# Two attention blocks on one core: row sums taken for two stretches at a time, and three smaller moves

## The chip, the cores and the metric

The kernel runs on one core of a Trainium2 chip. The metric is the device time in microseconds (us), median of the runs shown. The core has TensorE (PE), VectorE (DVE), ScalarE (ACT), GpSimd (POOL) and SyncE (SP), which here only issues DMAs. PE writes its results to PSUM[...] and DVE or ACT take them out. All data are fp32.

## The reference

Two residual attention blocks over `x` of shape (8, 512, 32, 32), 1024 tokens to an image.

```python
# layer 0: 32 groups, 8 heads of 64 channels
h = group_norm(x, gn_weight, gn_bias)
qkv = einsum('oc,bct->bot', w_qkv, h) + b_qkv
weight = softmax(einsum('bct,bcs->bts', q * scale, k * scale))
a = einsum('bts,bcs->bct', weight, v)
x = x + einsum('oc,bct->bot', w_proj, a) + b_proj
# layer 1: 8 groups, one head of 512 channels
xn = group_norm(x, gamma, beta)
attn = softmax(einsum('bqc,bck->bqk', q, k) * 512**-0.5)
x = x + conv1x1(attn applied to v, p_w, p_b)
```

## The kernel before

The images are worked through one after another. The period of an image is some 350 us. It holds the attention of layer 0 (`attention0`), the projection of layer 0, layer 1 of the image before (`layer1_scores`, `layer1_rest`), and the values, keys and queries of layer 0 for the image after. The 512 x 512 products use a seven-product scheme instead of eight (`wino`, `inner_steps`), whose sums and differences of factors are made by DVE and POOL.

**Attention of layer 0.** The eight heads are taken in four pairs `hp`, and the 1024 queries in two halves `tb`; pair and half make a stretch, eight to an image. The halves come in the order 0, 1, for the last pair 1, 0. In a stretch PE makes eight score tiles `sc` (128 keys, two heads, 512 queries). Each takes two PSUM banks of one of three pools, in turn (`ps_pools[n % 3]`). ACT takes the exponential to `e`, and DVE adds the eight `e` to a running sum `total` (called `sum` in the profile): the first add is line 623, the six others line 625. Then PE multiplies the `e` with the values into `av`, and ACT copies `av` to `a` without scaling it.

**Row sums.** `reciprocals` (line 575) is called right after. Four matmuls with a 128 x 32 block of ones sum `total` over the partitions (`sums`, 256 columns for four blocks of queries in four quadrants of the partitions). DVE makes the reciprocals from PSUM (line 586) and keeps their minimum in `low_recs` (line 587). POOL adds them to `all_recs` (line 588); both are looked at once, at the end of the kernel. Then SP's queue stores the reciprocals to DRAM (line 590) and reads them back in two broadcasts (line 600). POOL scales `a` with them (line 644); in the last stretch of an image that is done by DVE, and ACT's queue takes the DMAs. `av` and `sums` share a pool of two banks (`ps_acc`). The tiles `rc` and `r` have two buffers each.

**Order of the work.** All matmuls are pinned to the order of the text. The other engines' instructions are put in order by a planner, unless pinned too; with equal readiness the earlier in the text comes first. Short steps of other stages are handed to the stretches in lists (`extra`, one before and one after `av`): factors of the image for the next product (`t_h`, `h`, `t_a`) on DVE, and norms on ACT. In other stages short steps lie in a queue, `background`, from which each product takes one to four.

**Layer 1's scores** (`scores1`) are seven products of seven steps. Each puts its `small` steps in the queue: the steps `gsteps` of the factors of the scores, the 12 statistics `stats` of the projected image (eight half tiles, four ends), and `add_up`, POOL's sums of the exponentials.

**Keys and queries.** `keys_and_queries` runs `conv2` for keys, then for queries; each has four parts that take a list of hooks. The mean over groups (`group_mean`, a matmul of four columns and four small DVE instructions) and the scale (`affine`, one more such matmul, then DVE and POOL) are for the norm of a later image, whose statistics the values' stage makes.

Of the kernel before, what the change touches and what calls it, by code (L numbers as in the profile page):

```python
# [9 lines left out]
F32 = mybir.dt.float32  # L10
I32 = mybir.dt.int32
AF = mybir.ActivationFunctionType
ALU = mybir.AluOpType
AX = mybir.AxisListType

P = 128
# [13 lines left out]
def two_attention_blocks_kernel(  # L30
# [8 lines left out]
    nc = tc.nc  # L39
    B, C, T = x.shape  # L40
    KC = C // P
# [24 lines left out]
    def matmul(*args, **kw):  # L66
        tc.keep_in_program_order(nc.tensor.matmul(*args, **kw))  # L67
# [4 lines left out]
    def pcols(name):  # L72
        i = 4 * PARAMS.index(name)
        return par[:, i : i + 4]
# [101 lines left out]
    def main_path(ctx):  # L176
# [11 lines left out]
        def pair_tile(name):  # L188
            return big_tile(name, (P, 2, HT))

        def acc_tile(name):
            return ps_acc.tile([P, HT], F32, tag="acc", name=name)
# [379 lines left out]
            return out  # L572


        def reciprocals(total, uid, across, queue=nc.sync):

            sums = acc_tile(f"sums_{uid}")[:, : 2 * P].rearrange("p (a b) -> p a b", a=2)
            for i in range(4):
                matmul(sums[ts(i, 32), :, :], ones[:, :32], total[:, :, ts(i, P)], start=True, stop=True)
            rc = rpool.tile([P, 2, P], F32, tag="rc", name=f"rc_{uid}")
            nc.vector.reciprocal(rc, sums)  # L586
            nc.vector.tensor_tensor(low_recs, low_recs, rc, ALU.min)
            nc.gpsimd.tensor_tensor(all_recs, all_recs, rc, ALU.add)  # L588
            rows = rowpool.tile([2, 4, P], F32, tag="rows", name=f"rows_{uid}")
            queue.dma_start(rows.rearrange("j i n -> i j n"), rc[0:P:32, :, :])  # L590
            if across:
                r = pair_tile(f"r_{uid}")
                for j in range(2):
                    row = rows[j : j + 1].rearrange("j i n -> j (i n)")
                    queue.dma_start(r[:, j, :], row.to_broadcast([P, HT]))
            else:
                r = rpool.tile([P, HT], F32, tag="r", name=f"r_{uid}")
                for j in range(2):
                    row = rows[j : j + 1].rearrange("j i n -> j (i n)")
                    queue.dma_start(r[ts(j, 64), :], row.to_broadcast([64, HT]))  # L600
            return r


        def attention0(b, q, k, v, a, extra):
            n = 0

            for hp in range(KC):
                for tb in (0, 1) if hp < KC - 1 else (1, 0):
                    uid = f"0_{b}_{hp}_{tb}"
                    total = pair_tile(f"sum_{uid}")  # L610
                    es = []
                    for s in range(NS):
                        sc = ps_pools[n % 3].tile([P, 2, HT], F32, tag="sc", name=f"sc_{uid}_{s}")
                        n += 1
                        for j in range(2):
                            matmul(
                                sc[:, j, :], k[hp][ts(j, 64), ts(s, P)], q[hp][ts(j, 64), ts(tb, HT)],
                                start=True, stop=True,
                            )
                        e = pair_tile(f"e_{uid}_{s}")  # L620
                        nc.scalar.activation(e, sc, AF.Exp, scale=(C // 8) ** -0.5)  # L621
                        if s == 1:
                            nc.vector.tensor_add(total, es[0], e)  # L623
                        elif s > 1:
                            nc.vector.tensor_add(total, total, e)  # L625
                        es.append(e)
                    for f in extra.pop(0) if extra else ():
                        f()
                    av = acc_tile(f"av_{uid}")
                    for s in range(NS):  # L630
                        for j in range(2):
                            matmul(
                                av[ts(j, 64), :], v[s // 2][:, s % 2, hp * P + j * 64 : hp * P + (j + 1) * 64],
                                es[s][:, j, :], start=(s == 0), stop=(s == NS - 1),
                            )
                    for f in extra.pop(0) if extra else ():
                        f()
                    dst = a[hp][:, ts(tb, HT)]
                    nc.scalar.copy(dst, av)  # L639

                    last = (hp, tb) == (KC - 1, 0)
                    r = reciprocals(total, uid, False, nc.scalar if last else nc.sync)
                    if not last:
                        nc.gpsimd.tensor_tensor(dst, dst, r, ALU.mult)  # L644
                    else:
                        scaled = lambda dst=dst, r=r: tc.keep_in_program_order(nc.vector.tensor_mul(dst, dst, r))

            assert not extra
            return scaled


        def scores1(f, gf, gsteps, first, uid, stats):
# [26 lines left out]
            def exps(r, c):  # L679
                for cc in (1, 0):  # L680
                    nc.scalar.activation(e[c, cc, r], e[c, cc, r], AF.Exp, scale=scale)  # L681
# [11 lines left out]
            def product(s, p, y, x, before, small, after7=(), final=()):  # L693
                def mm(ps, j, start):
                    for i in range(2):
                        matmul(
                            ps[:, i, :], f[p][j][:, ts(i, P)], g2[p][j], start=start and i == 0, stop=True, skip_group_check=True
                        )

                def extra(r, cc, read, written):  # L700

                    if p == 6 and written:
                        more((0, 1), (1, 0), (1, 1), r, cc)
                    if p == 7 and written:
                        more((1, 1), (1, 0), (1, 1), r, cc)

                inner_steps(
                    f"{uid}_{s}", s % 2, 2, mm, add, lambda *at: blocks(y, *at), x and (lambda *at: blocks(x, *at)),
                    extra, after7, final, [lambda: background.extend(small), *(lambda q=q: factors(q) for q in before)],
                )  # L710

            product(0, 1, (1, 0), None, [2], stats[:3] + gsteps[:2])
            product(1, 2, (0, 0), (1, 0), [5], gsteps[2:4], (), [lambda: exps(0, 0)])
            product(2, 5, (1, 1), None, [6, 4], gsteps[4:] + stats[3:6])
            product(3, 6, (1, 0), (1, 0), [7, 3], stats[6:7])
            product(4, 7, (1, 0), (1, 0), [], stats[7:9])
            product(5, 3, (0, 1), (0, 1), [], stats[9:11] + add_up(0, 0), [lambda: exps(1, 1)], [lambda: exps(0, 1)])
            product(
                6, 4, (1, 0), (1, 0), [], stats[11:] + add_up(1, 1) + add_up(0, 1), (),
                [lambda: exps(1, 0), lambda: background.extend(add_up(1, 0) + steps)],  # L720
            )

# [229 lines left out]

        def keys_and_queries(b, f, norm, hooks):

            k = conv2("k", f, None, f"k0_{b}", hooks)
            hooks = [[all_background], [], []]
            if norm:
                hooks[1].append(lambda: norm.group_mean(acc_tile(f"gmean_0_{b + 1}")[:, :KC]))
                hooks[2].append(lambda: norm.affine(acc_tile(f"gvar_0_{b + 1}")[:, :KC]))
            q = conv2("q", f, pcols("bq0"), f"q0_{b}", hooks)  # L960
            return q, k

        def layer1_scores(b, inner):
# [9 lines left out]
        def layer1_rest(b, inner, gf, gsteps, stats, hooks, ahead):  # L973
            first = query_factors(gf[1], f"1_1_{b}")
            total, ef = scores1(inner, gf, gsteps, first, f"1_{b}", stats)
            state = {}

            def sums():
                state["r"] = reciprocals(total, f"1_{b}", True)

            z = by_token(
                weight("z"), hf, f"z1_{b}", hooks=[*hooks, [sums]], back=3,
                after=[load_weight, lambda: background.extend(zsteps)],
            )
            all_background()
            xt = [load_again(b, c, "x") for c in range(KC)]
            stiles = [big_tile(f"sz{i}_{b}", (P, 2, 2, C // 2)) for i in (1, 2, 4)]
            halves = lambda t: (t[:, :, : C // 2], t[:, :, C // 2 :])
            zf, zsteps = left_sums(
                [halves(t) for t in z[:2]], [halves(t) for t in z[2:]],  # L990
                [lambda j, t=t: t[:, j, :, :] for t in stiles], nc.vector.tensor_add, nc.vector.tensor_sub,
            )
            values1(b, zf, ef, state["r"], xt, f"1_{b}", ahead)
# [274 lines left out]
```

## Time and profile before

| what | us |
|---|---|
| median of 3 runs | 2849.69 (2848.17 to 2850.7) |
| the profiled execution | 2849.52 |
| its span, first to last instruction | 2847.7 |
| one stretch of attention, from sums to sums | 14.66 |
| PE busy in the span | 2827.0 (99%) |
| DVE busy | 2083.8 (73%) |
| POOL busy | 1205.4 (42%) |
| ACT busy | 929.0 (33%) |

Times in a timeline are counted from the start of the span. A line of it gives the start, the time, the engine, the line, the operation, what is written from what, and in brackets the idle time of the engine before it and what ended that. In a line of groups the two numbers behind the bar are the busy time in us and the mean of one in ns, then the idle time before. An fp32 matmul stands in the records as two instructions. Matmuls overlap in the records, so PE's pace is read from the starts.

### The profile page before, as it was taken

The numbers are of one execution on the slowest core, as the hardware profiler recorded it, in microseconds if no ns is written. First come the engines' busy times: TensorE is split into PE (matmuls) and PEld (weight loads), VectorE is DVE, ScalarE is ACT, GpSimd is POOL, SyncE is SP. The second block draws the span as 40 slices with busy tenths as digits, with TensorE's granted clock in tenths as the row PEclk, the third lists the DMA queues.
The fourth block names the chain that finished last, engine by engine and source line by source line (L and its number), as shares of the span: only waits on it lengthen the run. The fifth ranks groups of instructions, "written<-read, shape, count | busy, mean of one in ns | idle before, by whom it ended". The sixth has DMA issues, their size and how long they took to land.

```text
span 2847.7 us, 32456 instructions
## 1 busy us (share of the span) xinstructions
PE 2827.0 (99%) x11846; PEld 1690.0 (59%) x11846; DVE 2083.8 (73%) x2733; ACT 929.0 (33%) x1177; POOL 1205.4 (42%) x1193
## 2 busy tenths in 40 slices
PE   9999999999999999999999999999999999999998
PEld 5435635866367653677537674376743868338584
DVE  5587787766877678776787757877578775887765
ACT  1252452214522145220552215422154311633130
POOL 2123215732167321673227722277123761147672
PEclk9999999999999999999999999999999999999999
DMA  8632403133031230322213232122311223012301
GB/s 276 190 127 90 180 20 126 36 144 134 20 144 65 106 128 26 134 94 97 109 49 111 94 118 92 49 108 97 134 72 49 107 101 142 35 52 94 121 2 68
DMA packets 91597, 280.59 MB, mean 99 GB/s; under 512 B 10595, under 2 KB 36387, under 8 KB 82470
## 3 DMA queue, kind: packets, MB, share of 16 engines
q1 hardware_dynamic: 89638, 276.15, 26.7%
q10 hardware_dynamic: 1792, 2.29, 0.2%
q8 instruction: 96, 1.57, 0.2%
q14 instruction: 71, 0.58, 0.1%
HBM read 227.31 MB, written 51.09 MB: 98 GB/s over the span
## 4 chain that ended last, share of the span: by engine, by line
PE 97%; DVE 2%; issue 1%; ACT 0%; POOL 0%; DVEq 0%; POOLq 0%; ACTq 0%
PE sc L67 16%; PE av L67 16%; PE psb_av L67 6%; PE psb L67 5%; PE psa_av L67 4%; PE psc_av L67 4%; PE psc L67 3%; PE psa L67 3%; PE psb_z L67 3%; PE psb_p L67 3%; PE psb_v L67 3%; PE psb_k L67 3%; PE psb_g L67 3%; PE psb_q L67 2%; PE psa_p L67 2%; PE psa_z L67 2%
## 5 line engine op out<-in xcount | busy, mean ns | idle before, releaser
L625 DVE TENSOR_TENSOR sum<-sum,e 128x1024 f32<-128x1024 f32 x384 | 522.4, 1360 | 41.8 <-DVE sum L623 1.4
L621 ACT ACTIVATE e<-sc 128x1024 f32<-128x1024 f32 x512 | 476.8, 1053 | 73.2 <-PE sc L67 72.3
L67 PE MATMUL sc<-q,k 64*128 64x512 f32 x2048 | 458.7, 596 | 0.5
L67 PE MATMUL av<-e,v 128*64 128x512 f32 x2048 | 453.6, 596 | 0.0
L67 PEld LDWEIGHTS sc<-q,k 64*128 64x128 f32 x2048 | 193.3, 186 | 239.2 <-ACT e L621 104.0
L67 PEld LDWEIGHTS av<-e,v 128*64 128x64 f32 x2048 | 141.4, 137 | 304.3 <-issue 304.3
L588 POOL TENSOR_TENSOR all_recs<-all_recs,rc 128x256 f32<-128x256 f32 x72 | 65.2, 905 | 528.3 <-DVE rc L586 520.7
L644 POOL TENSOR_TENSOR a<-a,r 128x512 f32<-128x512 f32 x56 | 112.6, 2010 | 265.0 <-DMA r<-rows 220.8
L586 DVE RECIPROCAL rc<-sums 128x256 f32<-128x256 f32 x72 | 126.4, 1756 | 46.4 <-PE sums L67 26.5
L532 POOL TENSOR_TENSOR k<-k,k 128x256 f32<-128x256 f32 x28 | 20.0, 727 | 315.8 <-DVE u_k L527 315.8
L639 ACT COPY a<-av 128x512 f32<-128x512 f32 x64 | 37.4, 585 | 318.2 <-PE av L67 318.2
L623 DVE TENSOR_TENSOR sum<-e,e 128x1024 f32<-128x1024 f32 x64 | 78.5, 1226 | 58.9 <-ACT e L621 58.9
L67 PE MATMUL psb<-inner,inner_h 128*128 128x256 f32 x448 | 116.1, 382 | 1.2 <-DVE u L671 0.5
L67 PE MATMUL psa_av<-e,z 128*128 128x512 f32 x256 | 113.3, 596 | 0.0
L140 ACT ACTIVATE h<-h,b,s 128x1024 f32<-128x1024 f32 x62 | 78.4, 1268 | 93.9 <-DMA h<-in_x 77.3
L411 POOL TENSOR_TENSOR inner_h<-h,inner_h 128x256 f32<-128x256 f32 x120 | 106.8, 892 | 2.2
L67 PEld LDWEIGHTS psb<-inner,inner_h 128*128 128x128 f32 x448 | 83.9, 190 | 16.9 <-POOL inner L426 3.8
L411 POOL TENSOR_TENSOR inner_h<-h 128x256 f32<-128x256 f32 x60 | 58.8, 979 | 78.5 <-ACT h L140 78.5
L685 POOL TENSOR_TENSOR sum<-sum,e 128x1024 f32<-128x1024 f32 x32 | 76.2, 2380 | 27.5 <-ACT e L681 26.2
L67 PE MATMUL psb_g<-inner_h,w_m 128*128 128x256 f32 x336 | 86.0, 383 | 0.3
L411 POOL TENSOR_TENSOR inner_h<-t_h 128x256 f32<-128x256 f32 x90 | 77.9, 868 | 10.8 <-PE psc_av L67 9.5
L67 PEld LDWEIGHTS psa_av<-e,z 128*128 128x128 f32 x256 | 48.0, 190 | 57.2 <-issue 56.6
(344 smaller groups left out, 5535.4 us busy)
## 6 DMA issues: line engine op xcount, KB each, us to landing
x<-in_x SPq DMA_DIRECT2D x36, 512.0 KB
h<-in_x SPq DMA_DIRECT2D x32, 512.0 KB
spill<-x SPq DMA_DIRECT2D x32, 512.0 KB
h<-spill SPq DMA_DIRECT2D x32, 512.0 KB
x<-spill SPq DMA_DIRECT2D x32, 512.0 KB
out<-x SPq DMA_DIRECT2D x64, 256.0 KB
w_p<-sums_p SPq DMA_DIRECT2D x8, 1792.0 KB
r<-rows SPq DMA_DIRECT2D x112, 128.0 KB
```

The source lines that it names most:

```text
L67: tc.keep_in_program_order(nc.tensor.matmul(*args, **kw))
L140: tc.keep_in_program_order(nc.scalar.activation(dst, src, AF.Identity, bias=b, scale=s))
L411: pin(nc.gpsimd.tensor_tensor(dst, x, y, ALU.subtract))
L532: nc.gpsimd.tensor_tensor(d, x, y, ALU.add)
L586: nc.vector.reciprocal(rc, sums)
L588: nc.gpsimd.tensor_tensor(all_recs, all_recs, rc, ALU.add)
L621: nc.scalar.activation(e, sc, AF.Exp, scale=(C // 8) ** -0.5)
L623: nc.vector.tensor_add(total, es[0], e)
L625: nc.vector.tensor_add(total, total, e)
L639: nc.scalar.copy(dst, av)
L644: nc.gpsimd.tensor_tensor(dst, dst, r, ALU.mult)
L685: on = lambda dst, x, y: lambda: tc.keep_in_program_order(nc.gpsimd.tensor_tensor(dst, x, y, ALU.add))
```

## The change

Four things are changed.

1. `reciprocals` takes a list of totals. For pairs 0 and 1 the first half only keeps its total and its `a`; after the second half one call sums both totals into one bank, eight matmuls instead of four. What follows (reciprocal, minimum, `all_recs`, store, two broadcasts) is done for one total and then for the other, and then both halves of `a` are scaled. Pairs 2 and 3 are as before.
2. The pools of the score tiles are taken in the order 0, 2, 1.
3. In `scores1` some of the statistics come one or two products later.
4. Where `keys_and_queries` is called without hooks, `group_mean` moves from the second part of the queries to the first part of the keys, and `affine` from the queries' third part to the keys' fourth.

```diff
-        def reciprocals(total, uid, across, queue=nc.sync):
-            sums = acc_tile(f"sums_{uid}")[:, : 2 * P].rearrange("p (a b) -> p a b", a=2)
-            for i in range(4):
-                matmul(sums[ts(i, 32), :, :], ones[:, :32], total[:, :, ts(i, P)], start=True, stop=True)
-            rc = rpool.tile([P, 2, P], F32, tag="rc", name=f"rc_{uid}")
-            nc.vector.reciprocal(rc, sums)
...
+        def reciprocals(totals, uid, across, queue=nc.sync):
+            n = len(totals)
+            sums = acc_tile(f"sums_{uid}")[:, : n * 2 * P].rearrange("p (t a b) -> p t a b", t=n, a=2)
+            for t, total in enumerate(totals):
+                for i in range(4):
+                    matmul(sums[ts(i, 32), t, :, :], ones[:, :32], total[:, :, ts(i, P)], start=True, stop=True)
+            rs = []
+            for t in range(n):
+                rc = rpool.tile([P, 2, P], F32, tag="rc", name=f"rc_{uid}_{t}")
+                nc.vector.reciprocal(rc, sums[:, t, :, :])
+                nc.vector.tensor_tensor(low_recs, low_recs, rc, ALU.min)
+                nc.gpsimd.tensor_tensor(all_recs, all_recs, rc, ALU.add)
+                rows = rowpool.tile([2, 4, P], F32, tag="rows", name=f"rows_{uid}_{t}")
+                queue.dma_start(rows.rearrange("j i n -> i j n"), rc[0:P:32, :, :])
...
+                rs.append(r)
+            return rs
+
+        PAIRS_BEGUN = [(hp, 0) for hp in range(KC - 2)]
...
-                        sc = ps_pools[n % 3].tile([P, 2, HT], F32, tag="sc", name=f"sc_{uid}_{s}")
+                        sc = ps_pools[(0, 2, 1)[n % 3]].tile([P, 2, HT], F32, tag="sc", name=f"sc_{uid}_{s}")
...
-                    last = (hp, tb) == (KC - 1, 0)
-                    r = reciprocals(total, uid, False, nc.scalar if last else nc.sync)
-                    if not last:
-                        nc.gpsimd.tensor_tensor(dst, dst, r, ALU.mult)
...
+                    unscaled.append((total, dst))
+                    if (hp, tb) not in PAIRS_BEGUN:
+                        last = (hp, tb) == (KC - 1, 0)
+                        rs = reciprocals([t for t, _ in unscaled], uid, False, nc.scalar if last else nc.sync)
+                        for (_, dst), r in zip(unscaled, rs):
+                            if not last:
+                                nc.gpsimd.tensor_tensor(dst, dst, r, ALU.mult)
...
+                        unscaled = []
...
-            product(2, 5, (1, 1), None, [6, 4], gsteps[4:] + stats[3:6])
-            product(3, 6, (1, 0), (1, 0), [7, 3], stats[6:7])
-            product(4, 7, (1, 0), (1, 0), [], stats[7:9])
-            product(5, 3, (0, 1), (0, 1), [], stats[9:11] + add_up(0, 0), [lambda: exps(1, 1)], [lambda: exps(0, 1)])
+            product(2, 5, (1, 1), None, [6, 4], gsteps[4:] + stats[3:5])
+            product(3, 6, (1, 0), (1, 0), [7, 3], [])
+            product(4, 7, (1, 0), (1, 0), [], stats[5:7])
+            product(5, 3, (0, 1), (0, 1), [], stats[7:10] + add_up(0, 0), [lambda: exps(1, 1)], [lambda: exps(0, 1)])
             product(
-                6, 4, (1, 0), (1, 0), [], stats[11:] + add_up(1, 1) + add_up(0, 1), (),
+                6, 4, (1, 0), (1, 0), [], stats[10:] + add_up(1, 1) + add_up(0, 1), (),
...
-            k = conv2("k", f, None, f"k0_{b}", hooks)
-            hooks = [[all_background], [], []]
+            mean, affine = [], []
             if norm:
-                hooks[1].append(lambda: norm.group_mean(acc_tile(f"gmean_0_{b + 1}")[:, :KC]))
-                hooks[2].append(lambda: norm.affine(acc_tile(f"gvar_0_{b + 1}")[:, :KC]))
-            q = conv2("q", f, pcols("bq0"), f"q0_{b}", hooks)
+                mean.append(lambda: norm.group_mean(acc_tile(f"gmean_0_{b + 1}")[:, :KC]))
+                affine.append(lambda: norm.affine(acc_tile(f"gvar_0_{b + 1}")[:, :KC]))
+            if hooks:
+                k = conv2("k", f, None, f"k0_{b}", hooks)
+                q = conv2("q", f, pcols("bq0"), f"q0_{b}", [[all_background], mean, affine])
+            else:
+                k = conv2("k", f, None, f"k0_{b}", [[all_background, *mean], [], [], affine])
+                q = conv2("q", f, pcols("bq0"), f"q0_{b}")
```

More of the change, by code (lines that the diff above doesn't have):

```diff
@@ L572, in conv2 @@
             return out
-        def reciprocals(total, uid, across, queue=nc.sync):
-            sums = acc_tile(f"sums_{uid}")[:, : 2 * P].rearrange("p (a b) -> p a b", a=2)
-            for i in range(4):
-                matmul(sums[ts(i, 32), :, :], ones[:, :32], total[:, :, ts(i, P)], start=True, stop=True)
-            rc = rpool.tile([P, 2, P], F32, tag="rc", name=f"rc_{uid}")
[L586 to L601, printed above, removed]
@@ new lines, in reciprocals @@
+        def reciprocals(totals, uid, across, queue=nc.sync):
[12 more added lines that the diff above has]
+                queue.dma_start(rows.rearrange("j i n -> i j n"), rc[0:P:32, :, :])
+                if across:
+                    r = pair_tile(f"r_{uid}_{t}")
+                    for j in range(2):
+                        row = rows[j : j + 1].rearrange("j i n -> j (i n)")
+                        queue.dma_start(r[:, j, :], row.to_broadcast([P, HT]))
+                else:
+                    r = rpool.tile([P, HT], F32, tag="r", name=f"r_{uid}_{t}")
+                    for j in range(2):
+                        row = rows[j : j + 1].rearrange("j i n -> j (i n)")
+                        queue.dma_start(r[ts(j, 64), :], row.to_broadcast([64, HT]))
+                rs.append(r)
+            return rs
@@ L639, in attention0 @@
                     nc.scalar.copy(dst, av)
-                    last = (hp, tb) == (KC - 1, 0)
-                    r = reciprocals(total, uid, False, nc.scalar if last else nc.sync)
-                    if not last:
-                        nc.gpsimd.tensor_tensor(dst, dst, r, ALU.mult)
-                    else:
-                        scaled = lambda dst=dst, r=r: tc.keep_in_program_order(nc.vector.tensor_mul(dst, dst, r))
+                    unscaled.append((total, dst))
[5 more added lines that the diff above has]
+                                nc.gpsimd.tensor_tensor(dst, dst, r, ALU.mult)
+                            else:
+                                scaled = lambda dst=dst, r=r: tc.keep_in_program_order(nc.vector.tensor_mul(dst, dst, r))
+                        unscaled = []
             assert not extra
@@ L953, in keys_and_queries @@
         def keys_and_queries(b, f, norm, hooks):
-            k = conv2("k", f, None, f"k0_{b}", hooks)
-            hooks = [[all_background], [], []]
+            mean, affine = [], []
             if norm:
-                hooks[1].append(lambda: norm.group_mean(acc_tile(f"gmean_0_{b + 1}")[:, :KC]))
-                hooks[2].append(lambda: norm.affine(acc_tile(f"gvar_0_{b + 1}")[:, :KC]))
-            q = conv2("q", f, pcols("bq0"), f"q0_{b}", hooks)
+                mean.append(lambda: norm.group_mean(acc_tile(f"gmean_0_{b + 1}")[:, :KC]))
[3 more added lines that the diff above has]
+                q = conv2("q", f, pcols("bq0"), f"q0_{b}", [[all_background], mean, affine])
+            else:
+                k = conv2("k", f, None, f"k0_{b}", [[all_background, *mean], [], [], affine])
+                q = conv2("q", f, pcols("bq0"), f"q0_{b}")
             return q, k
@@ L978, in sums @@
             def sums():
-                state["r"] = reciprocals(total, f"1_{b}", True)
+                (state["r"],) = reciprocals([total], f"1_{b}", True)
             z = by_token(
```

## The prediction

> **What bounds the kernel now.** I read the busy table first, then the chain of waits, then the costliest groups, then the timelines of single stretches of the attention of layer 0.
>
> ```profile
> PE 2827.0 (99%) x11846; PEld 1690.0 (59%) x11846; DVE 2083.8 (73%) x2733; ACT 929.0 (33%) x1177; POOL 1205.4 (42%) x1193
> L625 DVE TENSOR_TENSOR sum<-sum,e 128x1024 f32<-128x1024 f32 x384 | 522.4, 1360 | 41.8 <-DVE sum L623 1.4
> L586 DVE RECIPROCAL rc<-sums 128x256 f32<-128x256 f32 x72 | 126.4, 1756 | 46.4 <-PE sums L67 26.5
> ```
>
> TensorE is busy 99% of the span, and the chain that ended last is 97% PE. So PE instructions count nearly one for one, and any wait of PE is lost time. DVE is at 73% on average, but the average hides the attention stage. There a stretch (one pair of heads, one half of the queries) lasts 14.66 us, and DVE has this to do in it. The timeline of DVE for the fourth stretch of image 1:
>
> ```profile
> 375.85 1.76 DVE L586 RECIPROCAL rc<-sums 128x256 f32<-128x256 f32 x1 [1.00 <-issue]
> 377.64 0.42 DVE L587 TENSOR_TENSOR low_recs<-low_recs,rc 128x256 f32<-128x256 f32 x1
> 378.81 1.23 DVE L623 TENSOR_TENSOR sum<-e,e 128x1024 f32<-128x1024 f32 x1 [0.74 <-ACT e L621]
> 380.14 8.76 DVE L625 TENSOR_TENSOR sum<-sum,e 128x1024 f32<-128x1024 f32 x6
> 388.82 0.69 DVE L1011 TENSOR_TENSOR t_h<-h,t_h 128x512 f32<-128x512 f32 x1
> ```
>
> PE's and GpSimd's timelines of the same stretch:
>
> ```profile
> 375.09 0.64 PE L67 MATMUL sums<-sum,ones 128*32 128x256 f32 x8
> 375.66 1.13 PE L67 MATMUL sc<-q,k 64*128 64x512 f32 x4
> ...
> 389.75 0.64 PE L67 MATMUL sums<-sum,ones 128*32 128x256 f32 x8
> ```
>
> ```profile
> 377.75 0.90 POOL L588 TENSOR_TENSOR all_recs<-all_recs,rc 128x256 f32<-128x256 f32 x1 [7.24 <-DVE rc L586]
> 382.91 2.25 POOL L644 TENSOR_TENSOR a<-a,r 128x512 f32<-128x512 f32 x1 [4.25 <-DMA r<-rows]
> ```
>
> The reader should see four things. A sums group holds PE 0.57 us (375.09 to 375.66). The last add ends at 380.14 + 8.76 = 388.90, and the sums that need it start at 389.75: a slack of 0.85 us. Before the first add DVE is idle 0.74 us, waiting for the second exponential. And six adds take 8.76 us although an undisturbed one takes 1.225: five come at 1.33 with their gap, and the one that meets GpSimd's scaling of `a` takes 2.12. A narrower window shows that one:
>
> ```profile
> 384.13 2.12 DVE L625 TENSOR_TENSOR sum<-sum,e 128x1024 f32<-128x1024 f32 x1
> ```
>
> So one scaling costs the adds 2.12 - 1.23 = 0.89 us. The trace of before even shows what happens when the slack is gone. In image 0 two scalings and one `all_recs` fall into the same seven adds (GpSimd, DVE and PE in turn):
>
> ```profile
> 171.49 1.73 POOL L644 TENSOR_TENSOR a<-a,r 128x512 f32<-128x512 f32 x1 [10.08 <-ACT e L621]
> 173.19 1.70 POOL L588 TENSOR_TENSOR all_recs<-all_recs,rc 128x256 f32<-128x256 f32 x1
> 174.85 2.24 POOL L644 TENSOR_TENSOR a<-a,r 128x512 f32<-128x512 f32 x1
> ```
>
> ```profile
> 169.53 9.98 DVE L625 TENSOR_TENSOR sum<-sum,e 128x1024 f32<-128x1024 f32 x6 [0.47 <-DVE sum L623]
> 179.42 1.29 DVE L1011 TENSOR_TENSOR t_h<-h 128x512 f32<-128x512 f32 x2
> ```
>
> ```profile
> 179.56 0.64 PE L67 MATMUL sums<-sum,ones 128*32 128x256 f32 x8 [0.72 <-DVE sum L625]
> ```
>
> The adds end at 179.51, the sums start at 179.56, and PE has stood still for some 0.7 us. This is the only such wait now.
>
> **What the skill says.** The Trainium skill, SBUF — State Buffer, section "SBUF: two separate sides", states that GpSimd and a DVE instruction with two SBUF inputs take turns at a shared port pair under an exclusive lock, held for the whole instruction. The trace agrees (2.12 against 1.23 us). By the same page the reciprocal, with one input and that from PSUM, would not be held up; the 1.76 us in all 72 agree. The Trainium skill, PSUM — Partial Sum Buffer, section "PSUM bank collisions raise a hardware error", says that PE may not write a bank while DVE reads the same partitions of it. So with both stretches' sums in one bank the first reciprocal has to follow the last of all eight matmuls; no run here shows that form yet. The Trainium skill, TensorE: Matmul & The Clock Gate, section "The mechanism" (packing), says that matmuls on different column tiles run together; in the trace the eight records of a group fit in 0.64 us, though one alone takes 0.39.
>
> **The change, part by part.**
>
> *Sums of two stretches at once, PE.* For pairs 0 and 1 the group after the first half goes, and the group after the second half has eight matmuls in place of four. Removed: 0.57 us. The switch from `av` to `sc` is still paid once. Added: four matmuls more, with the weights loaded behind. The eight records of a group start in two waves, and a group of two waves takes 0.57 us with one switch of about 0.1, so two further waves are about 0.48. Saved: 0.09 us for each of 16 pairs (8 images, 2 pairs), 1.4 us. The bounds are 0 and, if the added matmuls were free, 16 x 0.57 = 9 us; four column tiles are already full, so I exclude the second.
>
> *Two reciprocals in a row, DVE.* The number of reciprocals, `low_recs`, `all_recs`, DMAs (three to a stretch, on SP's queue) and scalings stays, but they come in twos at the start of the first half of pairs 1 and 2. At pair 1 this is covered: no sums follow its first half, so DVE may be late by up to a stretch's idle time. At pair 2 it isn't: the stretch (2, 0) has its own sums at its end. Step by step, in the times of the stretch above:
> - the second reciprocal with its minimum, 1.76 + 0.42 and two gaps of 0.03, is 2.24 us. It uses up the idle 0.74, less a gap of about 0.05: the first add is 1.55 late;
> - the second `all_recs` now meets the first add, where before it fell into the idle time. In image 0 an add that met one took some 0.35 more: 0.4;
> - the second scaling. Its rows are stored after the second reciprocal, and SP's queue sends them behind the first pair of broadcasts. In the trace 5.3 us pass from a reciprocal's end to its scaling (377.61 to 382.91 with the lock), so the second comes around 386, well inside the adds, which now last to 391: 0.89.
>
> Together 2.85 us late. Of the slack 0.85 about 0.06 is needed for the signal (179.51 to 179.56), so PE waits 2.85 - 0.79 = 2.05 us. Queued behind the waiting sums on PE is all of the next stretch, so nothing covers it. Eight images: +16.4 us. The bounds of one wait: 0.75 with only the first item, 2.3 with a longer meeting of `all_recs`. After the wait DVE has two factor steps of 0.69 to do ahead of the next reciprocal, which makes that some 0.6 us late; the idle 0.74 before the next first add takes it up.
>
> *Image 0's wait* of 0.7 us at (1, 1) should go, since no reciprocals stand before that half now: -0.7.
>
> *Order of the score banks* (0, 2, 1). At the head of each attention the second score tile takes the pool whose last drain is second to last. Now it waits for the last one: DVE drains `psb_q` until 680.40 (679.52 + 0.88), and the second tile starts some 0.2 us later than its turn. Seven images have this head: -1.4 us, between 0 and -2.
>
> *Statistics.* Three of layer 1's statistics move by one or two products towards the end. All are still made by about 535, ahead of the `gmean` matmul at 544.73; DVE's idle gaps of 0.2 to 0.9 us in the later products cover them. PE's waits in the first products are 0.2 to 0.3 us each, and the steps that make them stay. -0.5 us in all, between -1.5 and +1.
>
> *Norm of the image after next.* `gmean` moves from the second part of the queries to the first of the keys (five images), `affine` to the last. In image 2 the statistics end at 629.4, and the new place is reached at 636.4; DVE is idle 2.83 us there. The same matmuls (0.14 us of PE each) are paid elsewhere: 0. If the cover were gone, a late `x` tile would hold PE 1 to 5 us; the statistics' wait for it was at most 5.2.
>
> Sum against the profiled execution (2849.52 us; span 2847.7 and 1.8 around it): +16.4 - 1.4 - 0.7 - 1.4 - 0.5 = +12.4, so 2861.9. The runs shown have their median 0.2 above the profiled one; I say 2862.
>
> **Rivals.**
>
> *The pressure at (2, 0) is half as large* (chance 0.16). The second scaling slips past the adds or `all_recs` finds its gap: the wait is 0.75 to 1.2, say 1.0. Net 8 x 1.0 - 4 = +4, 2853.5. For it: GpSimd's times vary from stretch to stretch. Against: 386 lies five microseconds before the end of the adds.
>
> *The order on DVE differs: adds stand ahead of the second reciprocal* (chance 0.12), since the planner, and not the text, sets the order on engines that aren't pinned. Then nothing is late by more than the slack of 0.79 us, which is the point that decides, and only gains remain: -4, 2845.5. That is not slower. Against: in every stretch of before, DVE keeps the order of the text, reciprocal and minimum before adds.
>
> *Lateness spreads* (chance 0.10). The row sum of a first half lives a stretch longer in the 32 shared big tiles, or the lateness of (1, 0) runs into (1, 1), whose slack I put at 1.7 us. One more wait of 1 us or more in each image gives +22, 2872. Against: the waits list of before has no PE wait for a tile.
>
> **How the numbers follow.** My forecast has 0.62. No change can be told within 0.2%, 5.7 us. The forecast's own range, 1.6 to 2.3 us a wait, is 2857.5 to 2866. The range given, 2851 to 2868, takes in the first rival and leaves out the second, and most of the third. Slower: the forecast, the third rival and a part of the first, 0.79. Same: most of the first and of the second, 0.15. Faster: 0.06.
>
> **What would show it.** In the profile after: two reciprocals back to back twice in an image, the sums of (2, 0) starting some 2 us after the last `av`, with the end of DVE's adds just before; the stretch after a skipped group shorter by 0.57 us; the other stretches at 14.66. It would be wrong if the sums of (2, 0) start within 0.6 us of the last `av`, or if waits turn up in layer 1 or at `gmean`.

## The result, and the profile after

The changed kernel takes 2852.9 us (median of 20 runs, 2851.7 to 2855.2) where the kernel before takes 2849.1 beside it: a ratio of 1.0015 with the interval 1.0009 to 1.0020, or +3.8 us (2.6 to 5.7). The direction was forecast, the size was not: the forecast was +12.4, and 2862 us.

The profiled execution took 2852.07 us, with a span of 2850.3: +2.6 on the profiled one of before. Busy table, costliest groups and shares of the chain in the page of after:

```profile
PE 2822.1 (99%) x11846; PEld 1688.0 (59%) x11846; DVE 2080.1 (73%) x2733; ACT 928.6 (33%) x1177; POOL 1188.9 (42%) x1193
...
PE 94%; DVE 3%; ACT 1%; issue 1%; POOL 0%; DVEq 0%; ACTq 0%; POOLq 0%
...
L634 DVE TENSOR_TENSOR sum<-sum,e 128x1024 f32<-128x1024 f32 x384 | 520.7, 1356 | 41.4 <-DVE sum L634 0.5
```

The instruction counts are the same as before, PE is 5 us less busy, and its share of the chain fell from 97% to 94%: PE now stands still where DVE's adds are waited for. The list of PE's waits (engine, tile and line that waited, what for, us in total, times, longest) has a new head:

```profile
PE sums L67 <- DVE sum L634: 12.2, 8, 1.8
```

There was one such wait of 0.7 us before; now each of the eight images has one. PE's timeline of image 1, from the first half of pair 1 to the end of (2, 0):

```profile
374.06 7.14 PE L67 MATMUL sc<-q,k 64*128 64x512 f32 x32
381.12 7.09 PE L67 MATMUL av<-e,v 128*64 128x512 f32 x32
388.14 1.07 PE L67 MATMUL sums<-sum,ones 128*32 128x256 f32 x16
389.14 1.13 PE L67 MATMUL sc<-q,k 64*128 64x512 f32 x4
...
404.80 0.64 PE L67 MATMUL sums<-sum,ones 128*32 128x256 f32 x8 [1.50 <-DVE sum L634]
```

At 374.06 the scores of (1, 1) follow the `av` of (1, 0) with no sums between. The doubled group then holds PE 1.00 us (388.14 to 389.14). At 404.80 the sums of (2, 0) start late; the bracket puts it down to the adds. DVE's and GpSimd's timelines of the same stretch:

```profile
389.33 3.37 DVE L590 RECIPROCAL rc<-sums 128x256 f32<-128x256 f32 x2 [1.73 <-issue]
392.62 1.24 DVE L591 TENSOR_TENSOR low_recs<-low_recs,rc 128x256 f32<-128x256 f32 x2
393.78 1.21 DVE L632 TENSOR_TENSOR sum<-e,e 128x1024 f32<-128x1024 f32 x1
395.10 9.65 DVE L634 TENSOR_TENSOR sum<-sum,e 128x1024 f32<-128x1024 f32 x6
```

```profile
391.24 0.73 POOL L592 TENSOR_TENSOR all_recs<-all_recs,rc 128x256 f32<-128x256 f32 x1 [19.47 <-DVE rc L590]
392.85 0.73 POOL L592 TENSOR_TENSOR all_recs<-all_recs,rc 128x256 f32<-128x256 f32 x1 [0.88 <-DVE rc L590]
397.12 3.88 POOL L657 TENSOR_TENSOR a<-a,r 128x512 f32<-128x512 f32 x2 [3.55 <-DMA r<-rows]
```

Both reciprocals stand ahead of the first add, which starts 4.45 us after the first of them does (389.33 to 393.78) where it was 2.96 in the stretch shown of before. The planner did not keep the order of the text here: both reciprocals come first and then both minima, in all 16 places where two totals are summed at once. The first reciprocal starts behind the last of the eight matmuls (388.14 + 1.07 = 389.21), as the forecast had it. Both scalings (3.88 us) lie inside the six adds, which take 9.65 us instead of 8.76. The adds end at 404.75, and the sums follow at 404.80.

**How much one wait is.** From the start of the last wave of `av` to the start of the sums it is 0.52 us where nothing is late, and 2.09 in seven images of after: 1.57 us of waiting (1.83 in image 0). The length of the attention stage, from its first score matmul to the first matmul of its projection, repeats between executions to a few thousandths of a microsecond, so parts can be read from it alone: 117.576 us before, 118.525 after, +0.95 in seven images. In all eight it is +7.4 us. Yet the whole program is only 3.8 slower, so something outside this stage gets shorter. The experiments were made to take these two apart.

### The profile page after: what moved, and what is told of

Its sections match the earlier page's. It is cut to its first block, busy times and chain, and to the rows that moved or that the text cites. A ratio compares the mean times of both kernels' runs of the same rounds, so it can differ in the third digit from the quotient of the medians.

```text
span 2850.3 us, 32492 instructions
## 1 busy us (share of the span) xinstructions
PE 2822.1 (99%) x11846; PEld 1688.0 (59%) x11846; DVE 2080.1 (73%) x2733; ACT 928.6 (33%) x1177; POOL 1188.9 (42%) x1193
## 3 DMA queue, kind: packets, MB, share of 16 engines
q8 instruction: 96, 1.57, 0.2%
## 4 chain that ended last, share of the span: by engine, by line
PE 94%; DVE 3%; ACT 1%; issue 1%; POOL 0%; DVEq 0%; ACTq 0%; POOLq 0%
PE sc L67 14%; PE av L67 14%; PE psb_av L67 6%; PE psb L67 5%; PE psa_av L67 4%; PE psc_av L67 4%; PE psc L67 3%; PE psa L67 3%; PE psb_z L67 3%; PE psb_p L67 3%; PE psb_v L67 3%; PE psb_k L67 3%; PE psb_g L67 3%; PE psb_q L67 2%; PE psa_p L67 2%; DVE sum L634 2%
## 5 line engine op out<-in xcount | busy, mean ns | idle before, releaser
L592 POOL TENSOR_TENSOR all_recs<-all_recs,rc 128x256 f32<-128x256 f32 x72 | 57.4, 798 | 636.6 <-DVE rc L590 629.0
L657 POOL TENSOR_TENSOR a<-a,r 128x512 f32<-128x512 f32 x56 | 105.2, 1887 | 185.6 <-DMA r<-rows 159.9
```

## The experiments

Theory A is the forecast's account with the trace's sizes: the pairs make the loss through the wait at (2, 0), and the other parts give a little back. Where an expectation names a rival, its numbers stand beside A's. What was measured, each beside the kernel before on the same chip ("one run": a single execution, so no interval):

| kernel | us | ratio to before | attention, us an image | last DVE instruction to the end of the span, us |
|---|---|---|---|---|
| before | 2848.5 to 2849.4 | 1 | 117.576 | 6.96 |
| after | 2852.9 | 1.0015 (1.0009 to 1.0020) | 118.525 | 5.17 |
| e1_sums_only | 2858.3 | 1.0031 (1.0019 to 1.0043) | 118.866 | 7.06 |
| e2_banks_only | 2844.9 | 0.9985 (0.9978 to 0.9992) | 117.233 | 5.06 |
| e3_stats_norm_only | 2848.2 | 0.9997 (0.9989 to 1.0006) | 117.576 | 7.70 |
| e4_after_without_pairs | 2844.2 | 0.9981 (0.9973 to 0.9990) | 117.233 | 4.97 |
| e5_fill | 2846.6 | 0.9993 (0.9985 to 1.0002) | 117.576 | 5.08 |
| e6_scaling_on_vector | 2842.2 | 0.9979 (0.9971 to 0.9987) | 117.158 | 4.79 |
| e7_fewer_adds | 2841.1, one run | | 116.958 | 5.18 |
| e8_pair0_only | 2853.9, one run | | 118.616 | 5.01 |
| e9_scalings_apart | 2841.5 | 0.9972 (0.9961 to 0.9982) | 116.958 | 5.25 |

The attention column is the usual image; the first and now and then another differ a little.

**Each part alone.** The kernel before with one part of the change: the new `reciprocals` and `PAIRS_BEGUN`; the order of the banks; the lists of statistics with the hooks of the norm.

```diff
-                        sc = ps_pools[n % 3].tile([P, 2, HT], F32, tag="sc", name=f"sc_{uid}_{s}")
+                        sc = ps_pools[(0, 2, 1)[n % 3]].tile([P, 2, HT], F32, tag="sc", name=f"sc_{uid}_{s}")
```

> The paired sums alone; score banks, statistics and norm as before. Theory A (DVE is late at (2, 0), everything else is small and local): each attention stage is longer by the wait of 1.57 us less 0.28 us of PE saved at the two pairs, +1.29 us for images 1 to 7 (image 0 about +0.8, since its old wait of 0.79 goes and its new one is 1.8), all other stages unchanged: about +9.8 us, 2859. Theory B (the change saves some 3.5 us outside the stages, at the start and the end of the span, through the paired sums): about +6.3 us, 2855.5.

> Only the order of the score banks is changed. Theory A: the attention stage of images 1 to 7 is shorter by 0.34 us (0.95 measured for the whole change = 1.57 - 0.28 - 0.34), all else the same: -2.4 us. Rival: the 0.34 us belong to the paired sums, the bank order saves nothing (0 us), because the first score tile hides the drain.

> Only the statistics and the norm are moved. Theory A: keys +0.36 us and queries -0.37 us in the five images with a norm, scores of layer 1 0 to -0.35 us in an image; together 0 to -1 us. Theory B: it takes away the rare long waits of DVE seen in the one trace of before (an instruction of 7.8 us, PE losing 1.0 us in image 2) and so saves 2 to 4 us.

The pairs alone cost 9.45 us, the banks gain 3.9, statistics and norm are within the noise (-0.6). The three add up to +4.95, the whole change to +3.8, so within the noise the parts don't act on each other. In the trace of the pairs alone, the wait is the same as in after, but for image 0, where it is 0.25 us shorter:

```profile
PE sums L67 <- DVE sum L634: 12.0, 8, 1.5
```

The banks gained 1.5 us more than was expected of them. Their part in the attention is as A has it. The timeline of the weight loads at the head of image 2's attention, before and then with the new order:

```profile
679.35 0.30 PEld L67 LDWEIGHTS sc<-q,k 64*128 64x128 f32 x4 [0.33 <-issue]
680.52 0.33 PEld L67 LDWEIGHTS sc<-q,k 64*128 64x128 f32 x4 [0.87 <-PE sc L67]
```

```profile
679.90 0.30 PEld L67 LDWEIGHTS sc<-q,k 64*128 64x128 f32 x4 [0.33 <-issue]
680.44 0.19 PEld L67 LDWEIGHTS sc<-q,k 64*128 64x128 f32 x2 [0.24 <-issue]
```

Before, the second score tile's weights follow after 0.87 us of idle time, when DVE's drain of `psb_q` has ended at 680.40; in the new order after 0.24, since its bank was drained a step earlier. The view puts the 0.87 down to PE's own scores; but in the new order the weights start at 680.44 although the same drain still runs until 680.97, so it is the drain that they had waited for. The attention is 0.34 us shorter in seven images, 2.4 in sum. That leaves 1.5 of the 3.9.

**After without the pairs** is the change with `PAIRS_BEGUN` empty:

```diff
-        PAIRS_BEGUN = [(hp, 0) for hp in range(KC - 2)]
+        PAIRS_BEGUN = [(hp, 0) for hp in range(0)]
```

> The changed kernel with the list of begun pairs empty, so each half has its own sums again; banks, statistics and norm as changed. Theory A: no wait at (2, 0); attention -0.34 us an image, the rest as in the run with statistics and norm alone: -2.5 to -3.5 us, 2846. Theory B (the savings outside the stages come with the paired sums): 0 to -2.5 us; if they come with statistics and norm: -5 to -6 us.

It is 4.6 us faster than before (2.8 to 7.7), and the same attention as with the banks alone. So the pairs take the change from -4.6 to +3.8. The time fell by more than A had expected here, as with the banks alone.

**Where the rest of the banks' gain lies.** In the table's last column the kernels fall into two groups: some 7 us from DVE's last instruction to the end, or some 5. Those at 5 are, but for the fill that is told below, the ones with the new bank order. After the branch on `failed`, with which every one of these kernels skips its general path at the end, PE's queue has only a few instructions left, none of them a matmul. Its records of that branch and of the end (count, shortest, median and longest in ns, first and last start in us), before and then with the new bank order:

```profile
L1224 PEldq EVENT_SEMAPHORE  x1: 51/51/51, 2843.6 to 2843.6; - x1
L1264 PEldq DRAIN  x2: 8/8/8, 2847.0 to 2847.3; - x2
```

```profile
L1224 PEldq EVENT_SEMAPHORE  x1: 51/51/51, 2842.0 to 2842.0; - x1
L1264 PEldq DRAIN  x2: 8/8/8, 2842.2 to 2844.0; - x2
```

From the start of a semaphore instruction to that of the drain behind it 3.4 us pass before and 0.15 with the new order. Of these 3.2 us, 1.9 reach the end of the span; then SyncE is last. Its own drain ahead of the common end stands at 2845.06 before, 1.9 us ahead of PE's at 2846.98. The bank order puts seven more semaphore instructions into PE's stream (24092 records instead of 24085). If their number is what matters and not what they do, then anything that lengthens the stream a little should do the same. The fill puts three one-column matmuls ahead of the first weights (12 records more, loads included) and changes nothing else of before:

```diff
+            fill = acc_tile("fill")
+            for _ in range(3):
+                matmul(fill[0:1, 0:1], ones[:, :1], ones[:, 0:1], start=True, stop=True)
```

> The kernel before with three one-column matmuls into an unused tile ahead of the first transposes, where TensorE waits for the first load anyway; twelve instructions more in its stream, all other work unchanged. Theory A (the 1.9 us at the end depend on where the last instructions lie in TensorE's stream, and the new bank order moved them by its seven added semaphore instructions): the last barrier comes some 1.9 us sooner, 2847, and every stage keeps its length. Rival (the bank order itself frees something at the end): the tail stays at 7 us and the time at 2849.

The median falls by 1.9 us. The interval of the ratio reaches 1.0002, but 10 of the 13 runs with the fill lie below the fastest of the 27 beside them (2846.85), the attention is the same to a thousandth, and the trace shows the gap gone:

```profile
L1227 PEldq EVENT_SEMAPHORE  x1: 51/51/51, 2842.8 to 2842.8; - x1
L1267 PEldq DRAIN  x2: 8/8/8, 2843.1 to 2844.4; - x2
```

All eleven kernels agree: the three with 24085 records on PE have the long gap, the eight with 24092 or 24097 have the short one. Two edits that share nothing but a longer stream both remove it, so it isn't what the bank order does; that the place in the stream decides is well supported, though only three lengths were seen.

What PE waits for is argued from the times of the transfers. The Trainium skill, Runtime: NRT & Kernel Launch, section "Instruction fetch mechanics", says that the stream comes in 16 KiB blocks and that a branch taken out of the window waits for the fetch of the target's block. The branch itself takes 3.6 us on PE, and in all eleven traces two transfers of kind "instruction", 16 KiB each, fly at the end, the second 3.1 to 3.9 us after the first. The branch always ends 1.4 to 1.6 us after the first has landed. Where the gap is long, the drain starts 1.2 to 1.4 us after the second has landed (before: the two land at 2842.15 and 2845.78, the branch ends at 2843.55, the drain starts at 2846.98); where it is short, the drain starts before the second even sets out. So the long gap looks like a second wait of the same kind, for a block boundary right behind the target, but no run moved that boundary on purpose by single instructions.

**What the wait consists of.** If DVE's lateness in (2, 0) is the whole cause, fewer adds there must remove it. This kernel leaves the last two adds of (2, 0) out:

```diff
-                        elif s > 1:
+                        elif s > 1 and not ((hp, tb) == (2, 0) and s > 5):
```

> The changed kernel with the last two adds of the stretch (2, 0) left out in each image, so its row sums miss a quarter of the keys. Theory A (DVE's adds are what the sums of (2, 0) wait for): DVE is done 2.66 us sooner, the wait of 1.57 us is gone, attention 117.0 us in images 1 to 7, and the time 12 to 13 us shorter, 2840. Rival (the wait is for something else, a bank or the reciprocals): the sums of (2, 0) still start some 2 us after the last av.

PE's timeline of the same place as above:

```profile
402.25 0.64 PE L67 MATMUL sums<-sum,ones 128*32 128x256 f32 x8
```

No bracket: the sums follow the `av` at once, and the attention is 0.62 us shorter than before. That is what the parts give without the wait: 0.34 from the banks and 0.28 from two doubled groups of sums.

**Only pair 0** (`range(1)` in `PAIRS_BEGUN`) should move the wait to the next stretch with sums after a doubled group, and with it to (1, 0):

> The changed kernel with only pair 0 summed at once. Theory A (a wait comes wherever a stretch with sums of its own follows two reciprocals): the wait of 1.5 to 1.6 us moves to (1, 0) and the one at (2, 0) is gone; attention is 1.57 - 0.14 - 0.34 = +1.09 us longer than before in images 1 to 7. Rival (it belongs to pair 2's place, where more factor steps and norms run): no wait, attention 0.48 us shorter.

```profile
359.35 1.07 PE L67 MATMUL sums<-sum,ones 128*32 128x256 f32 x16
...
375.95 0.64 PE L67 MATMUL sums<-sum,ones 128*32 128x256 f32 x8 [1.45 <-DVE sum L634]
```

It did, with nearly the same size (2.04 less 0.52, 1.52 us), so one pair alone already pays the whole wait: in after the wait belongs to the first stretch behind pair 1, and pair 0's lateness is covered because no sums follow (1, 0).

**Taking the wait away.** Of the lateness, the second scaling holds a DVE add up by 0.87 us. Here DVE itself does the two scalings of pair 1, behind the adds of (2, 0):

```diff
-            unscaled = []
+            unscaled, late = [], []
...
+                    for f in late:
+                        f()
+                    late = []
...
-                            if not last:
+                            if hp == 1:
+                                late.append(lambda d=dst, r=r: tc.keep_in_program_order(nc.vector.tensor_mul(d, d, r)))
+                            elif not last:
                                 nc.gpsimd.tensor_tensor(dst, dst, r, ALU.mult)
```

> The changed kernel, but the two scalings of pair 1 are done by DVE, pinned after the adds of (2, 0), and not by GpSimd during them. Theory A (lateness 2.36 us at the last add, of which 0.87 from the second scaling and another 0.89 from the usual one): the adds of (2, 0) end 1.5 - 0.9 = 0.6 us later than in an ordinary stretch, inside the slack of 0.79, so the wait goes; each attention stage is 0.28 + 0.34 = 0.62 us shorter than before, and the time about 2842 to 2844, under both kernels. Rival (the two reciprocals alone make the wait, port contention matters little): a wait of 0.7 us or more stays at (2, 0) and the time is 2849 or above.

DVE's timeline, with the adds and the two scalings:

```profile
395.20 7.87 DVE L634 TENSOR_TENSOR sum<-sum,e 128x1024 f32<-128x1024 f32 x6
402.99 1.29 DVE L1035 TENSOR_TENSOR t_h<-h,t_h 128x512 f32<-128x512 f32 x2
404.19 1.29 DVE L660 TENSOR_TENSOR a<-a,r 128x512 f32<-128x512 f32 x2
```

The six adds take 7.87 us instead of 9.65, so the two scalings on GpSimd had cost them 1.78, and done by DVE they cost 1.21 (404.19 to 405.40), behind the adds. The wait at (2, 0) is gone (in one image 0.15 us are left), but every image got a new one of 0.2 to 0.4 us at (2, 1): the reciprocal of (2, 0) now starts two scalings later. So in the last kernel one scaling stands behind the adds of (2, 0) and the other behind those of (2, 1). Its edit against the kernel just shown:

```diff
-                    for f in late:
-                        f()
-                    late = []
+                    if late:
+                        late.pop(0)()
```

> As in the run with the scaling on DVE, but the second of the two scalings of pair 1 comes after the adds of (2, 1) and not of (2, 0). There, both together made the reciprocal of (2, 0) late and left a small wait of 0.2 to 0.4 us at (2, 1). Theory A (DVE's lateness is a sum of what is queued on it, stretch by stretch): half as much is queued, the wait at (2, 1) goes, attention is 117.0 us in images 1 to 7 (0.62 under before), and the time about 1.6 us under that run, 2840.5. Rival (the wait at (2, 1) comes from the next scaling on GpSimd alone): it stays, and the time is 2842.

```profile
402.15 0.64 PE L67 MATMUL sums<-sum,ones 128*32 128x256 f32 x8
...
416.81 0.64 PE L67 MATMUL sums<-sum,ones 128*32 128x256 f32 x8
```

No PE wait is left at either place, but for 0.15 us in one of the eight images. The attention is 116.958 us, the same as with the two adds left out, and here nothing is left out. At 2841.5 us it is 7.9 us (5.1 to 11.1) faster than the kernel before. It is the fastest kernel that leaves nothing out, though the interval of its ratio overlaps that of the kernel with both scalings together; the attention is 0.2 us shorter than there. Its eight attention stages together are 3.0 us shorter than without the pairs: that is what summing two stretches at once is worth when the wait is taken away.

## Why the prediction was wrong

Two steps failed. The wait at (2, 0) was priced at 2.05 us and is 1.57, because the second reciprocal with its minimum makes DVE 1.07 us late and not 1.55; and the end of the program, which got 1.8 us shorter, was left out of the sum, that is put at nothing without a reason. The banks and the sums of two at once gained 1.8 us more than forecast, which adds to this. The terms beside what the traces of after and before show, in us of the whole program:

| term | forecast | measured |
|---|---|---|
| wait at (2, 0), eight images | +16.4 | +12.8 (7 x 1.57 + 1.83) |
| image 0's old wait | -0.7 | -0.8 |
| sums of two at once, 16 pairs | -1.4 | -2.2 (16 x 0.14) |
| order of the banks | -1.4 | -2.4 (7 x 0.34) |
| statistics, with layer 1's scores | -0.5 | -0.6 (0.35 of it in one image, and only in kernels with pairs) |
| norm | 0 | 0 (keys +0.36, queries -0.37 an image) |
| end of the program | not in the sum | -1.8 |
| sum | +12.4 | +5.0, against 3.8 (2.6 to 5.7) in the runs |

*The mechanism was right*, but for the order of DVE's four short steps. Two reciprocals in a row, the sums of (2, 0) some 2 us behind the last `av`, the adds ending just before, nothing to cover it: each is in the trace. Fewer adds, another place for the scalings, or only one pair move the wait as this account says.

*The term that was mis-sized* is the first of the three, "the second reciprocal with its minimum". The lateness at (2, 0) was forecast as 1.55 + 0.4 + 0.89 = 2.85. It is 1.49 at the first add and 0.87 more over the seven adds with the second scaling (they take 10.96 us, and 10.09 before), 2.36 together. With the slack of 0.79, which was right, that makes 1.57.

The 1.49 holds two things. The second `all_recs` costs 0.42, close to the 0.4 of the forecast; only, it follows its reciprocal at once and meets the second minimum (0.84 us instead of 0.42; the two take 1.24), not the first add. What is left for the second reciprocal and its minimum is 1.07. The forecast had taken the order of the text, with a full length for each instruction and a gap behind it. The order on DVE is reciprocal, reciprocal, minimum, minimum. There the neighbours that don't need each other overlap by 0.08 us in the records: the first minimum starts at 392.62 and the reciprocals end at 392.70 (389.33 + 3.37), the add starts at 393.78 and the minima end at 393.86. Two reciprocals take 3.37 us, so the second adds 1.61 and not 1.79. Seven times 0.48 and 0.22 in image 0 are the 3.6 us that the first row is off.

*Sums of two at once* gained more: the doubled group takes 1.00 us, not the 1.05 that two further waves of 0.24 would give, 0.14 saved for each pair and not 0.09.

*The banks* gained 0.34 us at each head, not 0.2: the idle time ahead of the second tile's weights shrank by 0.63 us (0.87 to 0.24), and a little over half of that reached the stage. The estimate had counted only the 0.2 us by which the tile came after its turn.

*The end of the program* was not in the sum at all. The forecast followed the parts of the change to where they act; this gain comes, as far as the runs show, from where the last instructions of PE lie in its stream, and the bank order moved them. No view of before alone said which way it would go, but the 3.4 us gap was there to be seen.

*The rivals.* The time came out near the first rival's 2853.5, and so inside the range given, but that is luck: the second scaling did not slip past the adds, and the wait is not 1.0. The second rival (adds ahead of the second reciprocal) and the third (a further wait) are excluded by the timeline and the list of waits. The forecast's own range, 2857.5 to 2866, held neither a gain at the end nor several small terms that were all off to the same side.

The profiled executions differ by 2.6 us, and this is the account of it: attention +7.4, end -1.8, the start of the program -1.3, layer 1's scores -0.6, and -1.0 for a long wait of DVE that the last section shows, which the trace of before has and that of after has not. The start varies from 25.6 to 27.8 us between executions of these kernels, without relation to the change.

## What to carry to other kernels

Batching work on the bottleneck engine moves the follow-up work of the batch into one stretch; ask of the first stretch behind it, and not of the average, whether the engine that does the follow-up still makes its deadline. If it doesn't, move a step of it behind the deadline: two scalings put behind the adds turned +3.8 us into -7.9. And when differences of a few microseconds in 2850 are judged, measure the ends of the program apart from its stages.

## What the runs showed of the hardware

*Place in the instruction stream.* Twelve more records on PE, or seven, shorten the end of the program by 1.9 us (6.96 to 5.1), as told above; PE's branch over a skipped block takes 3.4 to 4.1 us in these kernels, and those of the other engines 0.05 to 0.07:

```profile
L1224 PEldq COMPARE_BRANCH  x1: 3607/3607/3607, 2839.9 to 2839.9; - x1
```

*Neighbours on DVE.* In the stretches shown, a DVE instruction that needs the result of the one right ahead of it starts 0.03 us (a minimum behind its reciprocal) to 0.10 us (an add behind an add) after that one's end; one that doesn't need it starts 0.08 us before that end. Two reciprocals in a row take 3.37 us, where one takes 1.76.

*GpSimd against DVE.* A GpSimd scaling of 128x512 holds the adds up longer (0.87 to 0.89 us) than the same scaling takes on DVE (0.61 with its gap), so moving it to the busier engine was a gain.

*A long wait of DVE.* In the profiled execution of before, one DVE product took 7.81 us instead of 0.69, while GpSimd ran an unbroken row of `inner_h` instructions of 0.72 us; PE lost 1.0 us by it. In DVE's timeline:

```profile
943.76 7.81 DVE L746 TENSOR_TENSOR o<-o,r 128x512 f32<-128x512 f32 x1
```

The exclusive lock that the Trainium skill, SBUF — State Buffer, section "SBUF: two separate sides", describes, would account for it if GpSimd got it back each time; that is argued and not shown. It isn't rare: eight of the eleven traces have the 7.8 us at this same product (all but after, `e3_stats_norm_only` and `e6_scaling_on_vector`), and two of these eight (`e1_sums_only`, `e9_scalings_apart`) have them once more at a later one. The moved statistics don't decide it, since kernels with them stand on both sides. Each kernel has one trace, so it stays open whether it belongs to the kernel or to the execution, and what starts it was not tested.
